# Order of loads and place of setup arithmetic in a four-layer graph network kernel

One Trainium2 chip, one core. The metric is the device time of one execution in microseconds (us), as the median of several runs. The profile is one further execution, taken by the hardware profiler; all its times count from the start of the span.

## The reference, cut

64 graphs of 256 nodes with 256 features pass through four layers of masked attention. Each layer's result is added to its input and normalised.

```python
x = _layernorm(x + _L0_gnn_ref(x, adj, Wq, bq, Wk, bk, Wv, bv, Wo, bo, gamma, beta))   # 4 heads of 64
x = _layernorm(x + _L1_gnn_ref(x, adj, gamma1, beta1, gamma2, beta2, W1, b1, W2, b2))  # 8 heads of 32, then an MLP
x = _layernorm(x + _L2_gnn_ref(x, adj, W, a))                                          # additive scores
x = _layernorm(x + _L3_gnn_ref(x, adj, a0, a1, a2, a3))                                # scaled dot scores
```

## The kernel before

The graphs run as 32 groups of two. Each group is a Python generator that is advanced piece by piece, and a new one enters every 15 steps, so that the layers of several groups alternate on the engines. TensorE's instructions are chained in the order of the program. Ahead of this loop stands setup, in one block: 23 loads, all issued by ScalarE, and arithmetic on weights that has four results. `bop` is bv times Wo plus bo. `wx` is L2's weights with three extra columns. `b2m` is b2 minus beta1, split into three bf16 rows. `bounds` are upper bounds that the last check compares with a limit.

```python
    def load_rows(name, cols):
        src = a[name]
        t = const.tile([P, src.shape[0] // P, cols], F32, name=name)
        nc.scalar.dma_start(t, src.rearrange("(c p) f -> p c f", p=P))
        return t
    # ... load_column, load_all: the same, on nc.scalar
    wqT = load_rows("L0_gnn_WqT", D)
    # ... 20 more loads, w1 and w2 (1 MB each) and b2 among them
    a12 = act.tile([P, 2, D], F32, name="a12", tag="z")
    nc.scalar.dma_start(a12, ...)
    # ... wa, wa1, the columns of wx
    rest = act.tile([P, D], F32, name="rest", tag="z")
    nc.vector.tensor_tensor(rest, b2, beta1r, ALU.subtract)
    part = act.tile([P, D], BF16, name="part", tag="y")
    for k in range(3):
        nc.vector.tensor_copy(part, rest)
        nc.sync.dma_start(b2m[k:k + 1, :], part[0:1, :])
        if k < 2:
            nc.vector.tensor_tensor(rest, rest, part, ALU.subtract)
    bvr = act.tile([P, NC, P], F32, name="bvr", tag="z")
    nc.vector.tensor_copy(bvr, bv.unsqueeze(2).to_broadcast([P, NC, P]))
    # ... product for bop; lengths; wsum
    nc.tensor.matmul(pm, ones, wsum, start=True, stop=True)
    # ... roots (a power on GpSimd), longest, bounds

    def group(g):
        x, adj = load_group(g)                       # two loads on SyncE
        yield
        adjb = io.tile([P, TB, N], BF16, name="adjb", bufs=1)
        nc.scalar.activation(adjb, adj, AF.Copy, accum_out=there[:, g:g + 1])
        # ... transposes of adjb with identb on TensorE, then the mask on VectorE
        xb, z = yield from layer0(g, x, mask)        # transposes of x; queries, keys, values; scores
        # ... layer1, layer2, layer3, store

    waiting = [group(g) for g in range(B // G)]
    next(waiting[0])
    running = []
    step = 0
    while waiting or running:
        if waiting and step % PACE == 0:             # PACE is 15
            running.append(waiting.pop(0))
            if waiting:
                next(waiting[0])
        for r in list(running):
            if next(r, END) == END:
                running.remove(r)
        step += 1
```

## Time and profile before

| before | value |
|---|---|
| time, median of 3 runs | 2787.66 us (2786.94 to 2789.51) |
| span of the profiled run | 2784.8 us |
| TensorE busy | 96% of the span |
| first transposes of group 0 on TensorE | 31.82 us |
| scores of group 0 start | 46.80 us |
| sums of its exponentials gathered (transposes of `zs`) | 56.36 us |

The prediction below shows the lines for the busy share, the first transposes and the start of the scores. For the last row, here are two lines of the timeline of the kernel before, VectorE and TensorE. In such lines PE is TensorE, DVE is VectorE, ACT is ScalarE and POOL is GpSimd; SPq and ACTq are the queues through which SyncE and ScalarE issue loads. The columns are start, duration, engine, line and operation, then output and inputs with a count, and in brackets the idle time before it and what ended it.

```profile
49.04 4.63 DVE L637 TENSOR_TENSOR e<-e,mask 128x1024 f32<-128x1024 f32 x4 [11.92 <-ACT e L635]
...
56.36 0.44 PE L570 MATMUL pm<-ident,zs 128*128 128x128 f32 x2
```

The four masking steps of layer 0's first scores take 4.63 us with nothing between them. From the start of the scores to the `zs` transposes it is 56.36 - 46.80 = 9.56 us. The `zs` transposes come after the last of the moved arithmetic that stands among the first group's work, and the order of TensorE is the same from there on. So the `zs` time is the mark at which I read what a start is worth.

### The profile page before, as it was taken

Reading aid. Unit: us, or ns where it says so; the run is one execution under the profiler, and the core shown is the slowest. Engines: PE = TensorE matmul, PEld = TensorE weight load, DVE = VectorE, ACT = ScalarE, POOL = GpSimd, SP = SyncE. Lnnn points to the kernel's source line nnn. Section 1 sums busy time; section 2 is a strip of 40 time slices with the busy share of each in tenths; the row PEclk is TensorE's granted clock in tenths of the full one; section 3 lists DMA queues with packets and bytes.
Section 4 is the critical chain, followed back from the end, with each engine's and each line's share of the span. In section 5 each row is a group of like instructions: output and inputs, shape, how many; then the busy total and the mean of one; then the engine's idle time right before and its main releaser. Section 6 shows DMA issues by size and latency. Waiting matters only on the chain.

```text
span 2784.8 us, 45617 instructions
## 1 busy us (share of the span) xinstructions
PE 2679.1 (96%) x17288; PEld 1842.6 (66%) x17288; DVE 1931.9 (69%) x6346; ACT 1295.8 (47%) x1953; POOL 578.4 (21%) x1138
## 2 busy tenths in 40 slices
PE   4899999999999999999999999999999999999996
PEld 2566666666667666667676667676666676666664
DVE  3666767776767776767776767777767777667764
ACT  2445445445444445444445444445444445444441
POOL 1112212212212212212212222212222212122211
PEclk9899999999999999999999999999999999999998
DMA  3000000000000000000000000000000000000000
GB/s 110 24 9 23 24 16 18 22 16 24 24 16 16 23 16 24 18 21 16 24 16 24 16 24 16 24 16 24 16 24 16 24 16 24 8 16 9 9 8 16
DMA packets 57905, 57.78 MB, mean 21 GB/s; under 512 B 5073, under 2 KB 57297, under 8 KB 57681
## 3 DMA queue, kind: packets, MB, share of 16 engines
q1 hardware_dynamic: 50784, 50.34, 5.9%
q10 hardware_dynamic: 6896, 4.47, 0.6%
q8 instruction: 139, 2.28, 0.3%
q14 instruction: 86, 0.70, 0.1%
HBM read 38.02 MB, written 16.78 MB: 20 GB/s over the span
## 4 chain that ended last, share of the span: by engine, by line
PE 68%; DVE 20%; POOL 8%; issue 2%; ACT 1%; DMA 1%; ACTq 0%; POOLq 0%; DVEq 0%
PE pm L567 53%; PE ps L567 9%; PE pm L570 6%; POOL rstd L590 6%; DVE xn L598 4%; DVE e L643 3%; DVE st L583 3%; POOL ve L586 2%; DVE z L598 1%; DVE mv L584 1%; DVE e L637 1%; ACT e L635 1%; DVE y L796 1%; DVE xb L802 1%; DVE xb L598 1%
## 5 line engine op out<-in xcount | busy, mean ns | idle before, releaser
L635 ACT ACTIVATE e<-ps 128x1024 f32<-128x1024 f32 x384 | 372.4, 1022 | 356.4 <-PE ps L567 353.3
L567 PE MATMUL pm<-L_gnn_W,hT 128*128 128x256 f32 x2048 | 463.2, 379 | 0.0
L567 PE MATMUL pm<-xT,L_gnn_W 128*128 128x512 f32 x1024 | 450.8, 593 | 0.0
L567 PEld LDWEIGHTS pm<-L_gnn_W,hT 128*128 128x128 f32 x2048 | 383.9, 190 | 63.2 <-issue 15.1
L643 DVE SCALAR_TENSOR_TENSOR e<-e,mask 128x256 f32<-128x256 f32 x1024 | 399.2, 453 | 29.2 <-ACT e L635 29.2
L840 ACT ACTIVATE hT<-pm,b 128x512 f32<-128x512 f32 x256 | 176.0, 688 | 477.8 <-PE pm L567 477.8
L586 POOL TENSOR_SCALAR ve<-mv 128x2 f32<-128x2 f32 x384 | 93.8, 244 | 1328.1 <-DVE mv L584 1131.9
L567 PEld LDWEIGHTS pm<-xT,L_gnn_W 128*128 128x128 f32 x1024 | 192.7, 191 | 216.6 <-issue 214.2
L590 POOL TENSOR_TENSOR rstd<-ve,mhalf 128x2 f32<-128x2 f32 (+1 forms) x384 | 298.4, 777 | 26.7
L583 DVE BATCH_NORM_STATS2 st<-y 128x6 f32<-128x256 f32 x768 | 299.8, 408 | 5.6
L598 DVE TENSOR_SCALAR xn<-y,mv,rstd 128x256 f32<-128x256 f32 x384 | 163.2, 471 | 127.6 <-POOL rstd L590 127.6
L923 DVE TENSOR_TENSOR qT<-qT,kT 128x1024 f32<-128x1024 f32 x32 | 39.2, 1225 | 195.2 <-ACT kT L922 195.2
L637 DVE TENSOR_TENSOR e<-e,mask 128x1024 f32<-128x1024 f32 x128 | 148.0, 1218 | 12.4 <-ACT e L635 12.4
L567 PE MATMUL pm<-e,z 128*32 128x256 f32 x2048 | 149.3, 385 | 3.5 <-DVE e L643 2.8
L567 PE MATMUL pm<-e,v 128*32 128x256 f32 x2048 | 135.5, 382 | 15.8 <-DVE e L637 15.8
L567 PE MATMUL ps<-xT 32*128 32x256 f32 x2048 | 148.0, 403 | 0.0
L826 POOL TENSOR_TENSOR both<-y,xb 128x512 f32<-128x512 f32 x64 | 81.7, 1276 | 313.2 <-DVE y L825 313.2
L764 POOL TENSOR_TENSOR x<-x,beta 128x1024 f32<-128x1024 f32 x32 | 75.7, 2365 | 324.7 <-PE pm L570 324.7
L616 ACT ACTIVATE xT<-pm,beta,gamma 128x512 f32<-128x512 f32 x128 | 92.9, 774 | 103.9 <-PE pm L570 103.6
L567 PE MATMUL ps<-qT,kT 64*128 64x256 f32 x1024 | 127.9, 389 | 0.6 <-ACT e L635 0.6
L567 PE MATMUL pm<-v,qT 128*128 128x260 f32 x512 | 120.3, 389 | 3.3 <-DVE qT L899 3.3
L567 PEld LDWEIGHTS ps<-xT 32*128 32x128 f32 x2048 | 93.3, 185 | 45.4 <-issue 42.1
(144 smaller groups left out, 4347.7 us busy)
## 6 DMA issues: line engine op xcount, KB each, us to landing
x<-in_x SPq DMA_DIRECT2D x32, 512.0 KB, 3.8
adj<-in_adj SPq DMA_DIRECT2D x32, 512.0 KB, 3.8
out<-xn SPq DMA_DIRECT2D x32, 512.0 KB, 2.9
L_gnn_W<-in_L_gnn_W ACTq DMA_DIRECT2D x2, 1024.0 KB, 7.3
L_gnn_WqT<-in_L_gnn_WqT ACTq DMA_DIRECT2D x1, 256.0 KB, 4.8
L_gnn_WkT<-in_L_gnn_WkT ACTq DMA_DIRECT2D x1, 256.0 KB, 6.7
L_gnn_WvT<-in_L_gnn_WvT ACTq DMA_DIRECT2D x1, 256.0 KB, 7.7
L_gnn_WoT<-in_L_gnn_WoT ACTq DMA_DIRECT2D x1, 256.0 KB, 8.9
```

The lines of the kernel that those rows point to most:

```text
L567: in_order(nc.tensor.matmul(*args, **kw))
L570: in_order(nc.tensor.transpose(*args))
L583: nc.vector.bn_stats(st[:, q, :], src[:, t, 0:D])
L586: nc.gpsimd.tensor_scalar(ve[:, 0], mv[:, :, 1], EPS, None, ALU.add)
L590: nc.gpsimd.tensor_tensor(rstd, ve, mhalf[:, 0:k * QB].rearrange("p (k t) -> p k t", k=k), ALU.pow)
L598: nc.vector.tensor_scalar(dst[:, t, 0:D], src[:, t, 0:D], mv[:, q, 0:1], rstd[:, q:q + 1], ALU.subtract, ALU.mult)
L616: nc.scalar.activation(dst[:, c, :], pt, AF.Identity, bias=bias[:, c:c + 1], scale=scale[:, c:c + 1])
L635: nc.scalar.activation(e, ps, AF.Exp, scale=scale)
L637: nc.vector.tensor_tensor(e, e, mask.unsqueeze(1).to_broadcast([P, 2, QB * N]), ALU.mult)
L643: nc.vector.scalar_tensor_tensor(e[:, h, k], e[:, h, k], 1.0, mask[:, k], ALU.mult, ALU.mult, accum_out=sums[:, kc, c, j:j + 1])
L826: nc.gpsimd.tensor_tensor(both[:, i * QB:(i + 1) * QB, 0:D], o, xi, ALU.add)
L840: nc.scalar.activation(hT[:, f, :], pm, AF.Gelu, bias=b1[:, f:f + 1])
```

## The change

The intent is to let group 0 start as soon as its own data is there. Its two loads go first on SyncE. ScalarE issues only the four loads that group 0's queries and keys need, and SyncE issues the others in order of use. The setup arithmetic becomes a generator of four pieces, advanced from step 5 on beside group 0. Its temporaries lie in one tile that shares the buffer of `hT`, the hidden layer of L1's MLP.

```diff
+PREPARE = 5
-    def load_rows(name, cols):
+    def load_rows(name, cols, queue=nc.sync):
...
-        nc.scalar.dma_start(t, src.rearrange("(c p) f -> p c f", p=P))
+        queue.dma_start(t, src.rearrange("(c p) f -> p c f", p=P))
...
+    setup = act.tile([P, NF, T], F32, name="setup", tag="hT", bufs=1).rearrange("p f t -> p (f t)")
...
+    first = load_group(0)
+    wqT = load_rows("L0_gnn_WqT", D, nc.scalar)
+    wkT = load_rows("L0_gnn_WkT", D, nc.scalar)
+    bq = load_column(a["L0_gnn_bq"], D, "bq", nc.scalar)
+    bk = load_column(a["L0_gnn_bk"], D, "bk", nc.scalar)
     wvT, woT, bv, bo, wx, a12, beta0, gamma0, beta1r, gamma1r, b2, columns   # cut: all on SyncE, in this order
+    second = load_group(1)
     w1 = load_rows("L1_gnn_W1", DFF)
     w2 = load_rows("L1_gnn_W2", D)
...
-        x, adj = load_group(g)
+        x, adj = (first, second)[g] if g < 2 else load_group(g)
...
+    def prepare():
+        ...                                     # bvr, the product with woT, bop
+        yield
+        ...                                     # wa, wa1, columns of wx
+        yield
+        ...                                     # b2m: three casts, three rows through SyncE
+        yield
+        ...                                     # squares, wsum, its product, roots, bounds
+    preparing = prepare()
...
         step += 1
+        if step >= PREPARE:
+            next(preparing, END)
```

More of the change, by code (lines that the diff above doesn't have):

```diff
@@ L446, in load_group, with load_column @@
         return x0, adj
-    def load_rows(name, cols):
+    def load_rows(name, cols, queue=nc.sync):
         src = a[name]
         t = const.tile([P, src.shape[0] // P, cols], F32, name=name)
-        nc.scalar.dma_start(t, src.rearrange("(c p) f -> p c f", p=P))
+        queue.dma_start(t, src.rearrange("(c p) f -> p c f", p=P))
         return t
-    def load_column(src, n, name):
+    def load_column(src, n, name, queue=nc.sync):
         t = const.tile([P, n // P], F32, name=name)
-        nc.scalar.dma_start(t, src.rearrange("(c p) -> p c", p=P))
+        queue.dma_start(t, src.rearrange("(c p) -> p c", p=P))
@@ L459, in load_column, with load_all @@
         return t
-    def load_all(src, name, tag=None):
-        t = act.tile([P, D], F32, name=name, tag=tag) if tag else const.tile([P, D], F32, name=name)
-        nc.scalar.dma_start(t, src.unsqueeze(0).to_broadcast([P, D]))
-        return t
-    wqT = load_rows("L0_gnn_WqT", D)
-    wkT = load_rows("L0_gnn_WkT", D)
+    setup = act.tile([P, NF, T], F32, name="setup", tag="hT", bufs=1).rearrange("p f t -> p (f t)")
+    def load_all(src, name, at=None):
+        t = const.tile([P, D], F32, name=name) if at is None else setup[:, at:at + D]
+        nc.sync.dma_start(t, src.unsqueeze(0).to_broadcast([P, D]))
+        return t
@@ L469, in usual_input @@
+    first = load_group(0)
[3 more added lines that the diff above has]
+    bk = load_column(a["L0_gnn_bk"], D, "bk", nc.scalar)
     wvT = load_rows("L0_gnn_WvT", D)
     woT = load_rows("L0_gnn_WoT", D)
-    bq = load_column(a["L0_gnn_bq"], D, "bq")
-    bk = load_column(a["L0_gnn_bk"], D, "bk")
     bv = load_column(a["L0_gnn_bv"], D, "bv")
-    bo = load_all(a["L0_gnn_bo"], "bo", "y")
+    bo = load_all(a["L0_gnn_bo"], "bo", 0)
@@ L475, in usual_input @@
+    wx = const.tile([P, NC, D + 3], F32, name="wx")
+    nc.sync.dma_start(wx[:, :, 0:D], a["L2_gnn_W"].rearrange("(c p) f -> p c f", p=P))
+    a12 = setup[:, 768:1280].rearrange("p (s d) -> p s d", s=2)
+    nc.sync.dma_start(a12, a["L2_gnn_a"].rearrange("(s f) o -> o s f", s=2).to_broadcast([P, 2, D]))
+    beta0 = load_all(a["L0_gnn_beta"], "beta0")
     gamma0 = load_all(a["L0_gnn_gamma"], "gamma0")
-    beta0 = load_all(a["L0_gnn_beta"], "beta0")
+    beta1r = load_all(a["L1_gnn_beta1"], "beta1r")
@@ L477, in usual_input @@
+    gamma1r = load_all(a["L1_gnn_gamma1"], "gamma1r", 256)
+    b2 = load_all(a["L1_gnn_b2"], "b2", 512)
     gamma1 = load_column(a["L1_gnn_gamma1"], D, "gamma1")
     beta1 = load_column(a["L1_gnn_beta1"], D, "beta1")
-    beta1r = load_all(a["L1_gnn_beta1"], "beta1r")
-    gamma1r = load_all(a["L1_gnn_gamma1"], "gamma1r", "y")
     gamma2 = load_column(a["L1_gnn_gamma2"], D, "gamma2")
     beta2 = load_column(a["L1_gnn_beta2"], D, "beta2")
+    b1 = load_column(a["L1_gnn_b1"], DFF, "b1")
+    a0 = load_column(a["L3_gnn_a0"], D, "a0")
@@ L483, in usual_input @@
+    second = load_group(1)
     w1 = load_rows("L1_gnn_W1", DFF)
-    b1 = load_column(a["L1_gnn_b1"], DFF, "b1")
     w2 = load_rows("L1_gnn_W2", D)
-    b2 = load_all(a["L1_gnn_b2"], "b2", "xn")
-    wx = const.tile([P, NC, D + 3], F32, name="wx")
-    nc.scalar.dma_start(wx[:, :, 0:D], a["L2_gnn_W"].rearrange("(c p) f -> p c f", p=P))
-    a12 = act.tile([P, 2, D], F32, name="a12", tag="z")
-    nc.scalar.dma_start(a12, a["L2_gnn_a"].rearrange("(s f) o -> o s f", s=2).to_broadcast([P, 2, D]))
@@ L493, in usual_input @@
-    wa = act.tile([P, 2, NC, D], F32, name="wa", tag="hT", bufs=1)
-    for s in range(2):
-        nc.vector.tensor_tensor(wa[:, s], wx[:, :, 0:D], a12[:, s:s + 1, :].to_broadcast([P, NC, D]), ALU.mult)
     wa1 = const.tile([P, 2, NC], F32, name="wa1")
-    nc.vector.tensor_reduce(wa1, wa, AX.X, ALU.add)
-    for k, (s, share) in enumerate(((0, SLOPE - 1.0), (1, SLOPE), (1, 1.0))):
-        nc.vector.tensor_scalar(wx[:, :, D + k:D + k + 1], wa1[:, s, :].unsqueeze(2), share, None, ALU.mult)
-    a0 = load_column(a["L3_gnn_a0"], D, "a0")
+    b2m = const.tile([P, D], BF16, name="b2m")
@@ L504, in usual_input @@
     onesb = const.tile([P, P], BF16, name="onesb")
-    nc.gpsimd.memset(onesb, 0.0)
-    nc.gpsimd.memset(onesb[0:3, :], 1.0)
-    b2m = const.tile([P, D], BF16, name="b2m")
-    nc.gpsimd.memset(b2m, 0.0)
-    rest = act.tile([P, D], F32, name="rest", tag="z")
-    nc.vector.tensor_tensor(rest, b2, beta1r, ALU.subtract)
-    part = act.tile([P, D], BF16, name="part", tag="y")
-    for k in range(3):
-        nc.vector.tensor_copy(part, rest)
-        nc.sync.dma_start(b2m[k:k + 1, :], part[0:1, :])
-        if k < 2:
-            nc.vector.tensor_tensor(rest, rest, part, ALU.subtract)
@@ L519, in usual_input @@
-    bvr = act.tile([P, NC, P], F32, name="bvr", tag="z")
-    nc.vector.tensor_copy(bvr, bv.unsqueeze(2).to_broadcast([P, NC, P]))
     bop = const.tile([P, D], F32, name="bop")
-    pm = ps_m.tile([P, D], F32, name="pm")
-    for c in range(NC):
-        nc.tensor.matmul(pm, bvr[:, c, :], woT[:, c, :], start=c == 0, stop=c == NC - 1)
-    nc.vector.tensor_tensor(bop, pm, bo, ALU.add)
     bounds = const.tile([P, 2], F32, name="bounds")
-    sq = act.tile([P, 2, D], F32, name="sq", tag="z")
-    nc.vector.tensor_tensor(sq[:, 0], gamma1r, gamma1r, ALU.mult)
@@ L531, in usual_input @@
-    nc.vector.tensor_tensor(sq[:, 1], beta1r, beta1r, ALU.mult)
-    lengths = const.tile([P, 4], F32, name="lengths")
-    nc.vector.tensor_reduce(lengths[:, 0:1], sq[:, 0], AX.X, ALU.max)
-    nc.vector.tensor_reduce(lengths[:, 1:2], sq[:, 1], AX.X, ALU.add)
-    wsq = const.tile([P, 2, NC], F32, name="wsq")
-    nc.vector.tensor_tensor(wsq, wa1, wa1, ALU.mult)
-    wsum = const.tile([P, 2], F32, name="wsum")
-    nc.vector.tensor_reduce(wsum, wsq, AX.X, ALU.add)
-    pm = ps_m.tile([P, 2], F32, name="pm")
@@ L540, in usual_input @@
-    nc.tensor.matmul(pm, ones, wsum, start=True, stop=True)
-    nc.vector.tensor_copy(lengths[:, 2:4], pm)
-    half = const.tile([P, 4], F32, name="half")
-    nc.gpsimd.memset(half, 0.5)
-    roots = const.tile([P, 4], F32, name="roots")
-    nc.gpsimd.tensor_tensor(roots, lengths, half, ALU.pow)
-    longest = const.tile([P, 2], F32, name="longest")
-    nc.vector.scalar_tensor_tensor(longest[:, 0:1], roots[:, 0:1], D ** 0.5, roots[:, 1:2], ALU.mult, ALU.add)
-    nc.vector.tensor_tensor(longest[:, 1:2], roots[:, 2:3], roots[:, 3:4], ALU.add)
@@ L549, in usual_input @@
-    nc.vector.tensor_scalar(bounds[:, 0:1], longest[:, 0:1], longest[:, 0:1], 32 ** -0.5, ALU.mult, ALU.mult)
-    nc.vector.tensor_scalar(bounds[:, 1:2], longest[:, 1:2], D ** 0.5, None, ALU.mult)
     def over_blocks(v, n=TB):
@@ L953, in group @@
         nc.sync.dma_start(out[g * G:(g + 1) * G].rearrange("b (q p) d -> p (b q) d", p=P), x[:, :, 0:D])
+    def prepare():
+        bvr = setup[:, 2560:2816].rearrange("p (c q) -> p c q", c=NC)
+        nc.vector.tensor_copy(bvr, bv.unsqueeze(2).to_broadcast([P, NC, P]))
+        pm = ps_m.tile([P, D], F32, name="pm")
+        for c in range(NC):
+            matmul(pm, bvr[:, c, :], woT[:, c, :], start=c == 0, stop=c == NC - 1)
+        nc.vector.tensor_tensor(bop, pm, bo, ALU.add)
+        yield
+        wa = setup[:, 1280:2304].rearrange("p (s c d) -> p s c d", s=2, c=NC)
+        for s in range(2):
+            nc.vector.tensor_tensor(wa[:, s], wx[:, :, 0:D], a12[:, s:s + 1, :].to_broadcast([P, NC, D]), ALU.mult)
+        nc.vector.tensor_reduce(wa1, wa, AX.X, ALU.add)
+        for k, (s, share) in enumerate(((0, SLOPE - 1.0), (1, SLOPE), (1, 1.0))):
+            nc.vector.tensor_scalar(wx[:, :, D + k:D + k + 1], wa1[:, s, :].unsqueeze(2), share, None, ALU.mult)
+        yield
+        nc.gpsimd.memset(onesb, 0.0)
+        nc.gpsimd.memset(onesb[0:3, :], 1.0)
+        nc.gpsimd.memset(b2m, 0.0)
+        left = setup[:, 2304:2560]
+        nc.vector.tensor_tensor(left, b2, beta1r, ALU.subtract)
+        part = setup[:, 3328:3456].bitcast(BF16)
+        for k in range(3):
+            nc.vector.tensor_copy(part, left)
+            nc.sync.dma_start(b2m[k:k + 1, :], part[0:1, :])
+            if k < 2:
+                nc.vector.tensor_tensor(left, left, part, ALU.subtract)
+        yield
+        sq = setup[:, 2816:3328].rearrange("p (s d) -> p s d", s=2)
+        nc.vector.tensor_tensor(sq[:, 0], gamma1r, gamma1r, ALU.mult)
+        nc.vector.tensor_tensor(sq[:, 1], beta1r, beta1r, ALU.mult)
+        lengths = const.tile([P, 4], F32, name="lengths")
+        nc.vector.tensor_reduce(lengths[:, 0:1], sq[:, 0], AX.X, ALU.max)
+        nc.vector.tensor_reduce(lengths[:, 1:2], sq[:, 1], AX.X, ALU.add)
+        wsq = const.tile([P, 2, NC], F32, name="wsq")
+        nc.vector.tensor_tensor(wsq, wa1, wa1, ALU.mult)
+        wsum = const.tile([P, 2], F32, name="wsum")
+        nc.vector.tensor_reduce(wsum, wsq, AX.X, ALU.add)
+        pm = ps_m.tile([P, 2], F32, name="pm")
+        matmul(pm, ones, wsum, start=True, stop=True)
+        nc.vector.tensor_copy(lengths[:, 2:4], pm)
+        half = const.tile([P, 4], F32, name="half")
+        nc.gpsimd.memset(half, 0.5)
+        roots = const.tile([P, 4], F32, name="roots")
+        nc.gpsimd.tensor_tensor(roots, lengths, half, ALU.pow)
+        longest = const.tile([P, 2], F32, name="longest")
+        nc.vector.scalar_tensor_tensor(longest[:, 0:1], roots[:, 0:1], D ** 0.5, roots[:, 1:2], ALU.mult, ALU.add)
+        nc.vector.tensor_tensor(longest[:, 1:2], roots[:, 2:3], roots[:, 3:4], ALU.add)
+        nc.vector.tensor_scalar(bounds[:, 0:1], longest[:, 0:1], longest[:, 0:1], 32 ** -0.5, ALU.mult, ALU.mult)
+        nc.vector.tensor_scalar(bounds[:, 1:2], longest[:, 1:2], D ** 0.5, None, ALU.mult)
```

## The prediction

> **What bounds the kernel now.** I read the page first: the busy table and the 40 slices.
>
> ```profile
> PE 2679.1 (96%) x17288; PEld 1842.6 (66%) x17288; DVE 1931.9 (69%) x6346; ACT 1295.8 (47%) x1953; POOL 578.4 (21%) x1138
> ...
> PE   4899999999999999999999999999999999999996
> ```
>
> TensorE is busy 96% of the span; every slice but the first, the second and the last is at 9. So TensorE is the bound, and setup can matter only in the first slices. The busy time of stretches puts a number on it: 2.08 us of TensorE work from 0 to 31.4 us, 69.80 of 70 us from 140 to 210 us, and 1771.90 of 1790 us from 210 to 2000 us. If the later order of work is unchanged, a microsecond gained before the first group's matmuls is a microsecond of the total.
>
> Next, the timeline of the first 60 us (start, duration, engine, line, what; in brackets the idle time before it and who ended it).
>
> ```profile
> 8.25 0.37 SPq L445 DMA_DIRECT2D adj<-in_adj  x1
> ...
> 22.01 1.28 ACT L934 ACT_TABLE_LOAD   x1 [22.01 <-DMA b<-in_L_gnn_b]
> 23.30 1.06 ACT L934 ACTIVATE adjb<-adj 128x1024 bf16<-128x1024 int32 x1
> ...
> 24.58 0.43 DVE L510 TENSOR_TENSOR rest<-b,beta1r 128x256 f32<-128x256 f32 x1 [22.43 <-DMA b<-in_L_gnn_b]
> 24.92 0.29 DVE L520 COPY bvr<-bv 128x256 f32<-128x256 f32 x1
> ...
> 31.40 0.56 PE L540 MATMUL pm<-wsum,ones 128*128 128x2 f32 x2 [4.06 <-DVE wsum L538]
> ...
> 31.82 1.01 PE L570 MATMUL pm<-identb,adjb 128*128 128x128 bf16 x8
> ...
> 34.36 1.75 PE L567 MATMUL pm<-xT,L_gnn_WqT 128*128 128x512 f32 x2
> ...
> 37.14 2.84 PE L567 MATMUL pm<-xT,L_gnn_WqT 128*128 128x512 f32 x6 [1.04 <-ACT xT L614]
> ...
> 46.80 2.00 PE L567 MATMUL ps<-qT,kT 64*128 64x256 f32 x16
> ```
>
> Two gates stand before group 0. ScalarE issues 23 loads itself, from 0.73 to 22.0 us, and only then casts the adjacency, although that had landed at 8.25 us (1.25 issue + 7.0, the largest time to landing of adj). Then TensorE, in its compiled order, must do two setup products (L524, L540) before the first transposes; the second waits for a VectorE chain that hangs on b2 (landed 24.5 us) and on L2's weights. So the first transposes start at 31.8 and the first projection at 34.36 us.
>
> The waits of TensorE say the same:
>
> ```profile
> PE pm L524 <- DVE bvr L520: 25.3, 1, 25.3
> ...
> PE pm L540 <- DVE wsum L538: 4.1, 1, 4.1
> ```
>
> **What the Trainium skill says.** "DMA: Bandwidth & Descriptors", section "Issuing engines are not separate DMA queues": loads issued from several engines share the same 16 DMA engines; more issuers save only sequencer time. The trace agrees: both queues together move 340 to 380 GB/s from 4.3 to 9 us, with x and adj on one, weights on the other. So moving loads to SyncE makes no bytes faster; it frees ScalarE and changes order. Same page, "Queues, rings and completion order": each DMA engine takes turns between the queues and consumes one queue's descriptors in order. The trace fits: WvT and WoT, issued at 1.82 and 2.37, land at 9.5 and 11.3 us, one after the other. "ScalarE: Activation LUTs", "What ACT_TABLE_LOAD costs": about 1283 ns; here 1.28 us. "TensorE: Matmul & The Clock Gate", "Part 1: The HAM clock gate": the array runs at half clock until about 3.4 us of sustained work. The trace has it: the first two projection pieces take 1.75 us (0.87 each), later ones 0.45 each. A cold start will be paid after the change too.
>
> **The change part by part.** I compared the compiled orders of both kernels. Apart from the first few dozen instructions, the orders of TensorE, VectorE, ScalarE and GpSimd are the same to the end. So I only have to time the start.
>
> *1. Loads.* ScalarE keeps four loads (WqT, WkT, bq, bk): some 2 us, and the table load is over before adj lands. SyncE issues x, adj, WvT, WoT, then bv, bo, wx, a12, broadcasts, columns, x and adj of group 1, w1, w2. Each issue waits for the landing of the one eight before it (compiled order; in the trace bk is issued at 5.56, when WqT lands at 5.5). WqT still lands near 5.5, so bv is issued there. It stands behind x, adj, WvT, WoT. Before, WoT landed at 11.3 behind 2.6 MB, group 1's x included; now the second x (0.52 MB, 1.45 us at 0.36 MB/us) is not ahead, so WoT lands near 9.8. Three bias columns landed 0.25 us apart before (11.6, 11.9, 12.1); bv then lands near 10.2 us.
>
> *2. VectorE's first instruction is now the copy of bv* (0.29 us), ahead of identb (0.52 us), and the first transposes need identb. So 10.2 + 0.1 + 0.7 = 11.0 us for the first transpose. ScalarE has adjb at 8.3 + 1.06 = 9.4: not the gate. Choice: I take the bv load as the gate.
>
> *3. First group.* From first transpose to first projection took 34.36 - 31.82 = 2.54 us: now 13.6. The four query matmuls took 39.82 - 34.36 = 5.46 us, with 1.04 idle because group 1's cast (1.06 us and a read) stood between the two copies of xT on ScalarE; in the new order the copies are adjacent: 4.5 us, to 18.1. The product for bop now lies here: 4 pieces, about 1.0 us between cold (0.634) and warm, to 19.1. Keys 3.44 us (43.26 - 39.82), to 22.5; values 3.54 us (46.80 - 43.26), to 26.1. Scores thus start at 26.1 instead of 46.8: **20.7 us earlier**.
>
> *4. Setup arithmetic beside it.* On VectorE, after the mask (12.3 to 13.5), the pieces sum to 1.29 + 1.21 + 8 x 0.3 to 0.42 + small ones, about 6 us: bop is ready near 19.6, and the second half of the values, which reuses its buffer, starts at 24.3. Hidden. What is not hidden lies among the four masking steps of the scores (1.15 us each, back to back before, from 49.04): after the first come the copy of lengths (0.16), a wait for GpSimd's power (1.03 + 0.15 + 0.04) and four small ones (0.5); after the second a third cast and three small ones (0.65). The fourth mask ends 2.5 us later in relation to the scores. TensorE needed it only at 54.73, about 1 us after it was ready (53.67); with wsum (0.5 us) among the scores, its product piece ends about **1.4 us later**. Nothing else is added after that.
>
> Sum: 20.7 - 1.4 = 19.3 us. 2787.7 - 19.3 = **2768.4 us**, ratio 1.007.
>
> **Rivals.**
> (a) *A new load wait takes the place of the old.* b2's split passes through SyncE: its first row is issued behind w1 and w2, and VectorE's second cast waits for it, ahead of the first mask of the scores. Before, all loads had landed at 25.8 us (a12: 21.02 + 4.8). The volume is nearly the same, so I expect 25 to 26; the first mask is due at 28.3. Against it: 2 us of slack. For it: in the before trace issuing b2 took 4.18 us behind w1 and w2, so the queue can stop the issuer. If it strikes, 2 to 6 us are lost: 2770 to 2775. The same holds for group 1's adj, now 21st in SyncE's order; ScalarE casts it between the two key copies, at 21.5; I expect it at 18 to 19.
> (b) *bv comes late*, because its 4-byte pieces lie behind big loads (6.1 us before) or SyncE's issue stalls: each us is lost one for one; 3 us late gives 2771.
> (c) *The gain is lost in later waits*: the first group alone is bound by VectorE's and GpSimd's chain (TensorE idle 8.6 us before L570 at 72.28), and the clock falls to 0.5 from 70 to 80 us. But that chain starts from the products and shifts with them; only the phase of the clock gate may differ by some us. If all were lost: 2788. The equal orders speak against it.
> (d) *The identity comes first anyway*: were the bv copy no gate, transposes could start at 9.5: 2767.
>
> **Range and chances.** The terms most at risk (bv's landing, the queued rows of b2, the clock's phase) are each 1 to 4 us, more of them downward than upward; the three runs before spread over 2.6 us. So 2763 to 2777. A 2% gain would need 2732, more than the whole 31 us before group 0; a loss of 2% has no mechanism here. Faster 0.005, same 0.99, slower 0.005.
>
> **What would show it.** Right: the first transpose of adjb near 11 us, ended by identb or bvr; scores at about 26; ScalarE's table load before 6; no idle of TensorE between the query matmuls; VectorE waiting for roots between the first masks, about 1.3 us; from 100 us on the same sequence, shifted by some 19 us. Wrong: a VectorE wait for b2m's load longer than 2 us before the first mask, ScalarE waiting for group 1's adj, or a steady part longer than before, which would mean that the equal orders ran differently.

## The result, and the profile after

Ratios here are the mean time of one kernel's fast runs over the mean of the other's fast runs of the same rounds, so they are not quite the ratio of the medians that I quote. They are changed over before; the 1.007 in the prediction is the other way up.

The changed kernel took 2765.58 us (2764.85 to 2766.6, 4 runs) against 2788.59 us (2786.94 to 2789.63, 4 runs) for the kernel before in the same rounds. The ratio is 0.9918, with a 95% interval of 0.9901 to 0.9935. That is 23 us or 0.8% less: clear of noise, but by the 2% rule the verdict is "same", as predicted. It is 2.8 us below the predicted 2768.4 and inside the range of 2763 to 2777.

| us from the span's start | before | after | earlier by |
|---|---|---|---|
| first transposes of the adjacency | 31.82 | 10.85 | 20.97 |
| first projection | 34.36 | 13.38 | 20.98 |
| scores start | 46.80 | 25.84 | 20.96 |
| transposes of `zs` | 56.36 | 36.82 | 19.54 |
| scores to `zs` | 9.56 | 10.98 | -1.42 |
| last check's product | 2777.13 | 2757.04 | 20.09 |
| span | 2784.8 | 2764.3 | 20.5 |

The page of the changed kernel, busy table and slices:

```profile
PE 2678.1 (97%) x17288; PEld 1842.3 (67%) x17288; DVE 1932.5 (70%) x6346; ACT 1294.7 (47%) x1953; POOL 576.8 (21%) x1138
...
PE   6999999999999999999999999999999999999986
```

The same work is done: the counts are those of before, and busy times differ by 2 us at most. The first two slices, 4 and 8 before, are now 6 and 9. The timeline of the changed kernel's first 40 us, lines of several engines in order of time:

```profile
8.33 1.06 ACT L888 ACTIVATE adjb<-adj 128x1024 bf16<-128x1024 int32 x1 [3.87 <-DMA adj<-in_adj]
10.36 0.29 DVE L913 COPY setup<-bv 128x256 f32<-128x256 f32 x1 [10.36 <-DMA bv<-in_L_gnn_bv]
10.57 0.22 DVE L418 CAST identb<-ident 128x128 bf16<-128x128 f32 x1
10.85 1.01 PE L524 MATMUL pm<-identb,adjb 128*128 128x128 bf16 x8 [10.85 <-ACT adj L889]
...
13.12 3.44 DVE L922 TENSOR_TENSOR setup<-wx,setup 128x512 f32<-128x512 f32 x2
13.38 4.77 PE L521 MATMUL pm<-xT,L_gnn_WqT 128*128 128x512 f32 x8
13.65 2.36 POOL L718 TENSOR_TENSOR x<-x,beta 128x1024 f32<-128x1024 f32 x1 [11.40 <-PE pm L524]
...
25.84 2.00 PE L521 MATMUL ps<-qT,kT 64*128 64x256 f32 x16
27.61 0.29 DVE L936 CAST setup<-setup 128x256 bf16<-128x256 f32 x1 [6.90 <-DMA b2m<-setup]
28.28 1.22 DVE L591 TENSOR_TENSOR e<-e,mask 128x1024 f32<-128x1024 f32 x1
30.77 0.16 DVE L961 SCALAR_TENSOR_TENSOR longest<-roots 128x1 f32<-128x1 f32 x1 [1.21 <-POOL roots L959]
31.16 1.21 DVE L591 TENSOR_TENSOR e<-e,mask 128x1024 f32<-128x1024 f32 x1
32.43 1.07 PE L521 MATMUL pm<-e,v 128*32 128x256 f32 x16 [0.85 <-DVE e L591]
36.82 0.44 PE L524 MATMUL pm<-ident,zs 128*128 128x128 f32 x2
```

What to see, from the top:

- The adjacency is cast at 8.33 us, not at 23.30. VectorE's first instruction waits for bv until 10.36; the cast of the identity stands behind it, and TensorE starts 0.06 us after that cast. The bracket names a ScalarE instruction as releaser, which ended at about the same time. Which of the two gates, experiment e3 decides.
- The four query matmuls (eight pieces in the trace) run without the idle 1.04 us that stood between them before.
- VectorE's two products with L2's weights take 3.44 us while a GpSimd addition runs.
- VectorE then waits 6.90 us for a row of `b2m` and is free only when the first mask is due, or a little later: that mask starts 2.44 us after the scores, before it was 49.04 - 46.80 = 2.24. After that mask it waits 1.21 us for GpSimd's power (`roots`), and TensorE waits 0.85 us for the second mask.

**The gain beyond 19.54 us.** After the first group the sequence is the same, and I followed the shift along the loads and stores of SyncE: 19.54 us at 70, 19.59 at 134, 19.58 at 261 and 20.12 at 2523 us (times of the kernel before), so nothing larger than some tenths comes after the start. Yet the timed medians are 23.0 us apart, and the spans 20.5. (The profiled run of the kernel before, 2786.67 us, was faster than its four timed ones.) Repeat profiles show why single numbers move. I ran the changed kernel again unchanged (after_again) and the kernel before again (before_again). The table of stretches shows the wait for `zs` of group 1 and what follows it; the columns are the stretch, its length, busy time and count of PE, PEld, DVE, ACT and POOL, then the granted clock, the DMA share and GB/s. Before:

```profile
114.00:119.00 5.00, 2.95 (x25) 2.27 (x18) 2.96 (x13) 1.27 (x3) 1.82 (x3) 0.86 0.00 2
119.00:125.00 6.00, 6.00 (x21) 3.92 (x20) 1.38 (x2) 3.36 (x4) 0.00 (x0) 0.83 0.00 0
```

The changed kernel, the same stretches 19.54 us earlier:

```profile
94.46:99.46 5.00, 2.97 (x27) 2.26 (x16) 2.98 (x13) 0.87 (x3) 1.83 (x3) 0.80 0.01 2
99.46:105.46 6.00, 6.00 (x23) 4.00 (x22) 1.29 (x2) 3.82 (x5) 0.00 (x0) 0.88 0.00 0
```

The changed kernel once more (after_again):

```profile
94.90:99.90 5.00, 2.97 (x34) 2.05 (x24) 3.11 (x14) 1.53 (x4) 1.86 (x3) 1.00 0.01 2
99.90:105.90 6.00, 6.00 (x23) 3.83 (x22) 1.55 (x3) 3.13 (x4) 0.00 (x0) 1.00 0.00 0
```

TensorE has the same 2 us pause in all three. In two runs the granted clock then falls; in the third it stays at 1.00, and there the shift against before goes from 19.07 to 20.58 us. So this one pause costs a run 1.5 us or nothing. The tail has a second such place, the score products of the last group's last layer (16 pieces). The timeline of the kernel before:

```profile
2756.36 5.35 PE L567 MATMUL ps<-z,xT 128*128 128x256 f32 x16 [0.41 <-ACT z L910]
```

and of before_again, the same program:

```profile
2756.63 6.96 PE L567 MATMUL ps<-z,xT 128*128 128x256 f32 x16 [0.41 <-ACT z L910]
```

Again 1.6 us or nothing, for identical instructions; from 2758 to 2762 us the granted clock was 0.81 in the one run and 0.50 in the other. With the value products after it, the tail took 2.16 us longer up to the last product (22.93 against 20.77). That is nearly all of the difference between the spans of the same kernel, 2784.8 and 2787.1 us: both paid in the middle, and before_again started 0.28 us later. Whether the change alters how often a run pays is not settled: eight of the twelve traces of all kernels ran slow in the middle (both of the kernel before, six of the other ten), three in the tail. So of the 23 us, 19.5 are shown at the start and 0.55 more along the way in one pair of traces. The rest is no larger than what the clock gives or takes from run to run; that the clock is its cause is not shown.

### The profile page after: what moved, and what is told of

Its sections match the earlier page's. It is cut to its first block, busy times and chain, and to the rows that moved or that the text cites. A ratio compares the mean times of both kernels' runs of the same rounds, so it can differ in the third digit from the quotient of the medians.

```text
span 2764.3 us, 45617 instructions
## 1 busy us (share of the span) xinstructions
PE 2678.1 (97%) x17288; PEld 1842.3 (67%) x17288; DVE 1932.5 (70%) x6346; ACT 1294.7 (47%) x1953; POOL 576.8 (21%) x1138
## 4 chain that ended last, share of the span: by engine, by line
PE 68%; DVE 20%; POOL 8%; issue 2%; ACT 1%; DMA 1%; POOLq 0%; SPq 0%; ACTq 0%; DVEq 0%
PE pm L521 53%; PE ps L521 9%; PE pm L524 6%; POOL rstd L544 6%; DVE xn L552 4%; DVE e L597 3%; DVE st L537 3%; POOL ve L540 2%; DVE z L552 1%; DVE e L591 1%; DVE mv L538 1%; ACT e L589 1%; DVE y L750 1%; DVE xb L756 1%; DVE xb L552 1%
## 5 line engine op out<-in xcount | busy, mean ns | idle before, releaser
L538 DVE BATCH_NORM_AGGREGATE mv<-st 128x2 f32<-128x6 f32 x768 | 121.6, 171 | 3.0
```

Of the source, the lines that this page charges most:

```text
L538: nc.vector.bn_aggr(mv[:, q, :], st[:, q, :])
```

## The experiments

All ten runs gave correct results. All ran in the fast state, except that before_again is a single timed run, whose state is unknown. e1 to e4 share one chip and 17 runs of the kernel before (2787.54 us; 2784.97 to 2791.28). after_again, e5, e6 and e7 share another chip and 9 runs of it (2788.09; 2785.46 to 2789.67). e8 and before_again ran on that chip later, with 8 runs (2787.52; 2785.67 to 2789.29).

The theory was that 20.9 us are gained by the order of loads and by the setup products leaving TensorE's way, and 1.4 us lost among the masks. Rival A: the loads alone bring nearly all of it. Rival B: moving the arithmetic alone does.

### e1: the new loads, the arithmetic in one block

```diff
     preparing = prepare()
+    for _ in preparing:
+        pass
```

> The new order and queues of the loads, but setup's arithmetic in one block ahead of the first group, as before. My theory (each microsecond before the first group's matmuls counts once, two gates in series): ScalarE is free early, but TensorE must do the setup product with wsum before the first transposes, and that waits for VectorE's chain on a12, beta1r, b2 and gamma1r, which landed at 12.7 to 15.7 us in the changed kernel. So wsum near 18.9, first transposes near 19.3 (changed kernel 10.85, before 31.8), scores near 33.3; about 13.5 of the profiled 19.5 us of gain, so 5 to 7 us slower than the changed kernel: 2770 to 2773. Rival A (freeing ScalarE from the loads is all there is): within 1.5 us of the changed kernel. Rival B (the pieces are all there is): within 3 us of the kernel before.

2772.81 us (2772.73 to 2773.63, 5 runs), ratio 0.9947 (0.9934 to 0.9961). TensorE's timeline in e1:

```profile
20.25 0.56 PE L521 MATMUL pm<-wsum,ones 128*128 128x2 f32 x2 [7.62 <-DVE wsum L952]
```

The setup product that the prediction named as second gate is still there and holds TensorE for 7.62 us, until VectorE has worked through the chain. The first transposes came at 20.67, scores at 35.10, `zs` at 44.66: 11.70 of the 19.54 us. Scores to `zs` took 9.56 us, as before, since no setup arithmetic lies between the masks. So the loads are worth 11.7 us and not all of it: rival A falls. The time lies in the expected 2770 to 2773, but the product with `wsum` was expected near 18.9 and the gain at 13.5 us.

### e2: the pieces, the loads as before

All loads go back to ScalarE in the order of before, and the two groups' loads stand after them in the program; only the arithmetic is spread.

```diff
-    def load_rows(name, cols, queue=nc.sync):
+    def load_rows(name, cols, queue=nc.scalar):
...
     a0 = load_column(a["L3_gnn_a0"], D, "a0")
+    first = load_group(0)
     second = load_group(1)
```

> Setup's arithmetic in pieces beside the first group, as in the change, but all loads through ScalarE in the old order. My theory: ScalarE issues loads until 22 us, then table load and cast, so first transposes near 24.5 us, 7.3 us before the 31.8 of the kernel before; the masks of the scores are disturbed as in the change (1.4 us). Gain 5 to 8 us: 2780 to 2783. Rival A: no gain, 2787 to 2789. Rival B: near the changed kernel, 2766 to 2768.

2785.74 us (2783.92 to 2786.84, 13 runs), ratio 0.9993 (0.9984 to 1.0001): no gain that can be told from noise, where I had expected 2780 to 2783. The start did move: the first transposes came at 24.70 us, 7.1 earlier. The timeline of e2, three engines:

```profile
28.65 1.37 DVE L936 CAST setup<-setup 128x256 bf16<-128x256 f32 x1
29.94 1.21 DVE L899 SCALAR_TENSOR_TENSOR mask<-pm,adjb 128x1024 bf16<-128x1024 bf16 x1
31.19 1.06 ACT L888 ACTIVATE adjb<-adj 128x1024 bf16<-128x1024 int32 x1 [3.98 <-DVE mask L899]
32.87 5.49 PE L521 MATMUL pm<-xT,L_gnn_WqT 128*128 128x512 f32 x6 [3.96 <-ACT xT L568]
46.21 2.00 PE L521 MATMUL ps<-qT,kT 64*128 64x256 f32 x16
```

Read it downward. VectorE's compiled order puts the mask of group 0 behind casts for `b2m`, and with the old loads b2 is late. ScalarE's order puts group 1's cast of the adjacency ahead of the second copy of `xT`. `adjb` has one buffer, so that cast waits 3.98 us for the mask to be done with it. TensorE waits 3.96 us for the copy. The scores start at 46.21 and `zs` at 56.80, 0.44 us later than before. A new wait took the place of the one removed. Rival B falls, and the two parts are not additive: the pieces bring 7.8 us on top of the new loads (19.5 - 11.7) and nothing without them, because in e2 VectorE does them ahead of the first group's mask and waits for b2, which landed at 24.76 us.

### e3: the identity ahead of bv

GpSimd takes over the copy of bv, so VectorE's first instruction is the cast of the identity. This is rival (d) of the prediction made real.

```diff
-        nc.vector.tensor_copy(bvr, bv.unsqueeze(2).to_broadcast([P, NC, P]))
+        nc.gpsimd.tensor_copy(bvr, bv.unsqueeze(2).to_broadcast([P, NC, P]))
```

> The changed kernel, with the copy of bv on GpSimd, so that VectorE's first instruction is identb. My theory: the load of bv (landed 10.3 us) was the gate of the first transposes; now ScalarE's cast of the adjacency is (9.4 us). First transposes near 9.5 instead of 10.85, the same 1.3 us from the total: ratio to the changed kernel 0.9995. If bv was no gate, or the gain is eaten by a later wait (b2m's first row landed at 27.6, the first mask follows at 28.28 and the scores' exponential ends at 28.1): first transposes early, but the scores' products at the same time as in the changed kernel, and no gain.

2767.31 us (2766.62 to 2770.16, 5 runs), ratio 0.9929 (0.9915 to 0.9942). The timeline of e3, TensorE and VectorE:

```profile
9.35 1.04 PE L524 MATMUL pm<-identb,adjb 128*128 128x128 bf16 x8 [9.35 <-ACT adjb L888]
...
28.01 0.29 DVE L936 CAST setup<-setup 128x256 bf16<-128x256 f32 x1 [6.31 <-DMA b2m<-setup]
28.68 1.22 DVE L591 TENSOR_TENSOR e<-e,mask 128x1024 f32<-128x1024 f32 x1
...
37.22 0.44 PE L524 MATMUL pm<-ident,zs 128*128 128x128 f32 x2
```

The transposes start 1.5 us earlier, so the copy of bv had been the gate, not the ScalarE instruction that the bracket named. The scores start at 24.29, also 1.55 us earlier. But the cast still waits for the row of `b2m`, until 28.01, and the first mask with it; `zs` comes at 37.22, no earlier than the 36.82 and 37.29 of the changed kernel's two traces. The gate had moved to the row's transfer, and the expected gain of 1.3 us did not come.

### e4: the bounds 40 steps later

```diff
         nc.vector.tensor_reduce(wsum, wsq, AX.X, ALU.add)
+        for _ in range(40):
+            yield
         pm = ps_m.tile([P, 2], F32, name="pm")
```

> The changed kernel, with the tail of setup's arithmetic (wsum's product, roots, bounds, which only the final check reads) 40 steps later. My theory: the 1.3 us wait for roots and the small ones between the first masking steps go, so the products of the first scores end about 1.2 to 1.4 us earlier against their start (the changed kernel: scores 25.84, first transposes of zs 36.82, so 10.98; before 9.56), and the total is 1 to 1.4 us less. Rival: that loss was not there or is absorbed at the next wait (8.6 us for rstd): the same time as the changed kernel within 0.5 us.

2766.67 us (2765.59 to 2768.07, 5 runs), ratio 0.9925 (0.9911 to 0.9939). VectorE's timeline in e4:

```profile
28.77 0.29 DVE L936 CAST setup<-setup 128x256 bf16<-128x256 f32 x1 [6.38 <-DMA b2m<-setup]
29.44 2.35 DVE L591 TENSOR_TENSOR e<-e,mask 128x1024 f32<-128x1024 f32 x2
```

The wait for `roots` between the masks is gone, and only the third cast stands between the second and the third. From the first mask to `zs` it took 6.59 us instead of 8.54. But the row landed later here (28.77), so scores to `zs` was 11.10 us, not the expected 9.6 to 9.8, and `zs` came at 36.03, only 0.8 us earlier; two traces of the changed kernel differ by 0.47 us there. Between 207 and 261 us, where the bounds now run, the shift fell from 21.82 to 20.90: 0.92 us was given back. In the timed runs no gain is left. What the move would bring with the row on time, this run can't say.

### after_again: the changed kernel once more

No edit.

> The changed kernel once more, unaltered, for a second trace and more times. Theory: all that the change does is over by the first transposes of zs (36.82 us; before 56.36, so 19.5 us), and what differs beyond that is the phase of the clock gate after the wait of 2.0 us for zs of group 1 (clock 0.80 and 0.88 in two traces' stretches there, 1.00 in three others, worth 1.5 us), which falls one way or the other from run to run. So zs at 36.8 again within 0.3, and the rest of the span (2727.5 us in the first trace) anywhere from 2726 to 2729. Rival (the change also makes the steady part shorter): the rest stays below the 2728.4 of the kernel before whatever the clock does.

2765.60 us (2764.72 to 2767.01, 5 runs), ratio 0.9921 (0.9908 to 0.9935): the result repeats, 22.5 us under the kernel before in the same rounds. `zs` came at 37.29, where 36.8 within 0.3 had been expected. Its trace has the cast for `b2m` at 28.07 and the first mask at 28.75, where the changed kernel's first trace had 27.61 and 28.28; scores to `zs` took 11.85 us instead of 10.98. The scores themselves began at 25.44, 0.40 us earlier, so that against them the cast was 0.86 us later and `zs` 0.87. So the row's landing reaches TensorE nearly one for one, and the 2 us of slack that the prediction gave it are not there.

### e5: e3 with a tile of its own for each row

With three tiles for the parts, no cast waits for the transfer of the part before it.

```diff
-        part = setup[:, 3328:3456].bitcast(BF16)
         for k in range(3):
+            part = setup[:, 3328 + k * 128:3456 + k * 128].bitcast(BF16)
```

> The identity-first kernel, with a tile of its own for each of the three parts of b2's split, so that VectorE no longer waits for a row's landing (28.0 us there) before the first mask. Theory: the 1.55 us that the earlier transposes gained at the scores (24.29 instead of 25.84) now reach the products: first transposes of zs near 35.3 instead of 37.22 (changed kernel 36.82), total 1.5 us under the changed kernel. Rival: another load holds the same place (group 1's adjacency, cast on ScalarE ahead of the second key copy, landed at 22.2), and zs stays above 36.

2764.76 us (2763.4 to 2765.96, 4 runs), ratio 0.9916 (0.9901 to 0.9931). `zs` came at 35.81, 1.4 us earlier than in e3, where 35.3 had been expected; scores to `zs` fell from 12.93 to 11.80. The rival struck in part: ScalarE waited for group 1's adjacency until 22.55, the second half of the scores then waited 0.46 us for the keys, and the first mask came 3.46 us after the scores. The wait for the row is removed and its worth seen in the trace; in the timed runs 0.8 us against the changed kernel lies within the spread.

### e6: e5 with the bounds after the last group

```diff
+        yield "last"
         pm = ps_m.tile([P, 2], F32, name="pm")
...
-        if step >= PREPARE:
+        if PREPARE <= step < PREPARE + 4:
             next(preparing, END)
+    next(preparing, END)
```

> As the one before, and the tail of setup's arithmetic (wsum's product, roots, bounds) after the last group. Theory: masks back to back again, zs 9.56 us after the scores as in the kernel before, so near 33.9; total 2.5 to 3 us under the changed kernel, less what the tail costs at the end (at most 1 us). Rival: in the run with bounds 40 steps later, 0.95 us came back between the third and fourth group; the same may come back at the end.

2764.26 us (2763.62 to 2765.61, 5 runs), ratio 0.9916 (0.9902 to 0.993). The four masks take 4.63 us with nothing between, as before the change, and `zs` came at 34.67 (33.9 expected: group 1's cast on ScalarE delayed the second copy of the keys). But of the 22.34 us by which the last load was early, 20.42 were left at the last check's product. The bounds cost about 1.5 of these 1.9 us: from the last value products to the check's product it took 12.06 us, in the kernel before 10.60. In timed runs e6 is 1.3 us under the changed kernel, in overlapping spreads.

### e7: group 0 as early as its data

On top of e6: the adjacency is loaded ahead of x, WqT and WkT go through SyncE, the biases through ScalarE. An order without a wait puts the other setup arithmetic after `bop` and group 1's cast after group 0's exponentials.

```diff
-    first = load_group(0)
-    wqT = load_rows("L0_gnn_WqT", D, nc.scalar)
+    first = load_group(0, True)                    # adj before x
+    wqT = load_rows("L0_gnn_WqT", D)
...
+        if g == 1:
+            after(cast, exps[3])
...
+            after(nc.vector.tensor_tensor(wa[:, s], ...), of_bop)
```

> As the one before, with the adjacency and then x as the only first loads (all big loads on SyncE in order of use, the bias columns on ScalarE), bop ahead of the other setup arithmetic on VectorE, and group 1's cast after the exponentials of group 0's scores. Theory: what bounds the start is now the landing of x, 1.05 MB at some 0.36 MB/us, near 6.0 us instead of 8.2, then transposes near 6.2, first projection near 8.1, scores near 20.5, zs near 30: 6 to 7 us under the changed kernel, some 2759. Rival: a weight or a small load comes late (WqT behind x), and the gain is under 4 us.

2761.37 us (2760.03 to 2761.78, 4 runs), ratio 0.9905 (0.989 to 0.992). Its runs lie wholly below those of the changed kernel in the same rounds (2764.72 to 2767.01). TensorE's timeline in e7:

```profile
6.63 1.03 PE L532 MATMUL pm<-identb,adjb 128*128 128x128 bf16 x8 [6.63 <-ACT adjb L896]
7.86 1.94 PE L532 MATMUL pm<-ident,x 128*128 128x128 f32 x8 [0.19 <-DMA x<-in_x]
...
21.20 2.00 PE L529 MATMUL ps<-qT,kT 64*128 64x256 f32 x16
30.76 0.44 PE L532 MATMUL pm<-ident,zs 128*128 128x128 f32 x2
```

The adjacency is cast at 5.43 instead of 8.33, and x, now second, ends a short wait at 7.86. Scores to `zs` is 9.56 us again, all of the loss between masks removed. `zs` is 6.06 us earlier than in the changed kernel; of these 2.06 are lost again at the end (the shift falls from 26.37 to 24.31), 1.48 of them in the stretch with the bounds. The timed 4.2 us agree with that difference. The 2759 us expected were missed: that sum had no term for the bounds.

### e8: e7 with the bounds beside the last group

```diff
-        if PREPARE <= step < PREPARE + 4:
+        if PREPARE <= step < PREPARE + 4 or not waiting and len(running) == 1:
             next(preparing, END)
-    next(preparing, END)
```

> The early-start kernel, with the tail of setup's arithmetic in the first step in which the last group runs alone, instead of after it. Theory: at the very end it stood in the chain that ends the kernel (the shift against the kernel before fell from 26.37 us at the last load to 24.31 at the final product, 2.06 us); in the last group's own waits it is hidden. So the shift at the final product is 26 or more, the total 1.5 to 2 us less than the early-start kernel, near 2759.5. Rival: it costs the same wherever it stands, and the total stays at 2761.4 within 0.7.

2761.51 us (2760.91 to 2763.99, 5 runs), ratio 0.9907 (0.9893 to 0.9921): the same as e7. From the transposes of the last group's layer 2 exponentials to the last product its tail took 40.20 us against 39.54 in before_again, both with the slow score products. The same stretch took 39.12 in e7 against 37.42 before, both with the fast ones. That is 0.66 instead of 1.7 us for the bounds in single traces, a hint that half or more of them hide there. The timed runs don't show it, and the 2759.5 us expected did not come, so it stays open. e7 and e8 are equally the best versions.

### before_again: the kernel before once more

No edit.

> The kernel before, unaltered, for a second trace. Theory of the clock's phase: scores at 46.8 and first transposes of zs at 56.4 as before, and the granted clock after the 2.0 us wait for zs of group 1 (near 115 to 125 us) either again below 1 with a rest of the span of about 2728 to 2729 us, or 1.00 with a rest 1.5 us shorter. Rival (the kernel before has a steady part that is longer by 1 to 2 us whatever the clock does): clock 1.00 there and a rest above 2728.

One run, 2789.01 us. `zs` at 56.64, within 0.3 us of the first trace, and the last product at 2779.56, 2.43 us later. The granted clock was low after the pause here too (0.66 from 117 to 122 us), and the tail's score products were the slow ones shown above.

## Why the prediction was right, point by point

**The bound.** Right. TensorE is busy 97% and what was gained ahead of the first group stayed gained: 19.54 us at `zs`, 20.09 at the last product.

**The two gates.** Right, and e1 and e2 show that both had to go: loads alone 11.7 us, pieces alone nothing, both 19.5.

**Landing of bv and the copy ahead of the identity.** Right: 10.36 against 10.2 to 10.3 for the copy and 10.85 against 11.0 for the first transposes. e3 shows that this copy was the gate. Rival (d) was right that the transposes would start at about 9.5 without it (9.35), but wrong in what it made of the time: e3 is no faster than the changed kernel, and that its 2767.31 us fit the 2767 of rival (d) is luck.

**The first group up to the scores.** Right: projection 13.38 against 13.6, scores 25.84 against 26.1, a gain of 20.96 against 20.7. The half clock at the start is read from the length of the first pieces (0.87 us against 0.45); the clock column of both traces shows 1.00 there, so that the clock made them slow is not shown.

**Among the masks.** The sum was right, 1.42 us against 1.4, but in part by luck: 0.20 us of it is the first mask's delay by the row, and 1.22 fell between that mask and `zs`. e5 and e6, which differ only in the bounds, confirm the cause: from the first mask to `zs` they took 8.34 and 7.31 us (the kernel before 7.32). In e1 and e7, with no setup arithmetic between the masks, scores to `zs` is 9.56 us. And a term was mis-sized in the setup arithmetic ahead of it: 7.6 us on VectorE, from 13.12 to 20.7, not 6. The two products with L2's weights took 3.44 us beside GpSimd's addition, and 1.29 in e3 and in after_again, where they ran ahead of it. It cost nothing that the traces show: VectorE waited for the row anyway, and the row was not sooner where it was issued sooner (see the next point).

**Rival (a), the row of b2m.** This step failed in size. I expected the landing at 25 to 26 us with 2 us of slack; the wait lasted 6.90 us and ended at 27.61, so the slack was about nil. The prediction counted the volume and not the rate. Two stretches of the changed kernel (columns as in the tables above, the last is GB/s):

```profile
13.00:18.00 5.00, 5.00 (x12) 2.29 (x11) 5.00 (x7) 1.60 (x3) 2.36 (x1) 1.00 0.80 75
18.00:27.60 9.60, 9.60 (x45) 6.59 (x43) 2.67 (x13) 5.98 (x10) 0.00 (x0) 1.00 1.07 371
```

From 13 to 18 us, while the short column loads went through, only 75 GB/s moved. w1 and w2 were issued at about 17 us; in the kernel before it was 14.63 and 15.68. So the row, issued behind them at 18.85, was late. Five traces agree: w1 was issued at 16.97 us in the changed kernel, 17.74 in after_again, 17.94 in e1, 17.98 in e3 and 18.40 in e4, and the wait for the row ended at 27.61, 28.07, 28.01, 28.01 and 28.77. When the row itself was issued counted less: 19.08 in e1 and 19.84 in e3, with the same end. No run moves w1 and w2 by themselves. Two of the prediction's own signs of being wrong appeared, this wait and ScalarE's for group 1's adjacency. That the total held is luck: the wait ended just as the mask was due. In after_again it ended 0.86 us later against the scores, and `zs` came 0.87 later. Had it been another 2 us later, the prediction would have been off by as much. Group 1's adjacency also came later than the expected 18 to 19: ScalarE waited for it until 21.88, 0.42 us idle.

**Rival (b)** did not strike; bv landed as expected. **Rival (c)** was right in its second half only: the waits after the first group moved with the products, and the clock's phase gives or takes 1.5 us in the middle and 2.2 in the tail.

**The sum.** 19.3 predicted, 19.54 measured at the start. The timed gain is 3.5 us more than that. The prediction had no term for it other than the phase of the clock, which it counted in the range and not in the sum; so the fit of the total to 2.8 us leans on a wide range. Two places where runs pay or do not are shown; that the kernel before pays more often is not.

## What to carry to other kernels

When one engine is busy to 96%, look at the slices where it is not: here the first 32 us, which setup held with loads that the first group didn't need and products that waited for the last of them. Moving the arithmetic pays only when its operands land early too, and every piece put between the first group's steps can hold an engine that works in its compiled order: check what stands behind each new wait (a shared temporary, a single buffer) before counting its cost as hidden. Where effects of 1 or 2 us are asked for, mark a point early in the trace and compare that, since whole runs of one program differ by more. The mark too should be taken twice: `zs` repeated within 0.28 and 0.47 us here.

## What the Trainium skill lacked or had wrong

- "TensorE: Matmul & The Clock Gate", "Part 1: The HAM clock gate": it says that the cold ramp varies from run to run and costs under 1% of a span. The runs fit: the slow stretches after a pause cost 1.5 us in the middle and 2.2 us in the tail, 0.1% together. What it lacks is that this hides small edits: the kernel before alone ranges from 2784.97 to 2791.28 us, and e3 to e6 differ from the changed kernel by less than 2 us.
- "SBUF — State Buffer", "SBUF: two separate sides": it says that VectorE and GpSimd share a port pair as an exclusive lock held for a whole instruction, also where VectorE reads two SBUF inputs. This fits: the pair of products took 3.44 us beside a GpSimd addition of 2.36 us and 1.29 us without it, and a square that takes 0.42 us in e7 took 1.17 in e3 and 1.67 in e4, where it ended 0.28 and 0.29 us after the addition that it overlapped. The page gives no sizes for such pairs.
- No page gives a size for how long a small transfer waits behind large ones: a row of 0.5 KB, issued at 18.85 us after two loads of 1 MB, ended VectorE's wait at 27.61, 8.8 us later.
